# Eleven block products for twelve: Strassen's algorithm for pairs of output chunks in a q, k, v projection

## The chip, the cores and the metric

The kernel runs on one core of a Trainium2 chip. The metric is the device time of one execution in microseconds. Engines are named as in the profile: PE (TensorE), PEld (its weight loads), DVE (VectorE), ACT (ScalarE), POOL (GpSimd), SP (SyncE, here only a queue for transfers). Each has its own in-order queue; they meet at semaphores. On-chip memory is SBUF, the memory that TensorE writes to is PSUM[...].

## What is computed

Everything is float32. Two layers in a row on x of 384 channels and 192 x 192 pixels; this case concerns the first half of the first one:

```python
qkv = jnp.einsum('bchw,oc->bohw', gn(x), w_qkv) + b_qkv      # 384 -> 1152 channels, every pixel
qkv = qkv.reshape(b, 3*c, 96, 2, 96, 2).max(axis=(3, 5))      # 2 x 2 max pooling
qkv = depthwise_conv3x3(qkv, w_dw) + b_dw                     # on 96 x 96
q, k, v = split(qkv); q, k = normalized along the pixels
attn = q @ k.T * temperature                                  # 8 heads, 48 x 48
out = sum of four top-k softmaxes (k = 24, 32, 36, 38) of attn, each @ v * a_i
x = x + project(upsample(gelu(out)))
```

After it comes a second layer of depthwise convolutions (13 x 13 and six smaller ones, merged into one), on the normalized x.

## The kernel before, in words

**Tiling.** Channels are cut into chunks of 128: x has 3 (index j), the output has 9 (m: q is 0 to 2, k is 3 to 5, v is 6 to 8). Rows are cut into 24 blocks B of 8 input rows, each block into two halves (sb) of 4 input rows, 2 pooled rows. A half of a block and one output chunk is a *step*: it needs 2 x 384 columns (r = 0, 1: two input rows each) from 3 input chunks, six products of 128x128 by 128x384, summed in two PSUM banks (`project`, L665).

**Passes.** First x is read once for the statistics of the normalization (L301 to L585); what is already known of chunks 0 and 1 is used meanwhile for 18 early steps of blocks 0 to 5 (chunks m = 0 to 2, sb = 0), whose sums over j = 0, 1 are kept in SBUF (`put_by`) and put back into a bank by ACT just ahead of their step (`fill`, L264). Sums of 2 x 2 pixels of x (`sum_up`, L278) are made by POOL for a later stage; those of the early pieces that are left over are worked off at L636, behind the clearing of the nine padded tiles (L631 to L634). Then the q and k pass goes over the 24 blocks, 12 steps each (B 0 to 23), and the v pass once more over the same 24 blocks, 6 steps each (B 24 to 47), with the attention (`attend`, L797, mostly small DVE work) stepped on between its products. Then come the product of attention and v (L1131), the projection (L1459) and the second layer (L1371 to L1412).

**A step.** TensorE's six products; a DVE reduction takes the maximum over 2 x 2 pixels from the two banks (`pool`, L681 to L683); ACT adds the bias on the way into the padded tile of that chunk (L690). When both halves are there, ACT begins the depthwise sum with the middle tap (`begin`, L703), DVE adds the other eight taps (`taps`, L719), and ACT squares the result for the norms and copies the two last rows up (`end`, L733, L738). For q and k, TensorE transposes the result (`turn`, L748), ACT copies it (L750), and TensorE adds to the gram matrix (`add_gram`, L760).

**Order.** Nothing is reordered by a scheduler (`manual_schedule`): the order of the calls is the order on every engine's queue. The loop (L1006) issues a step's first product, then what is due at this step (`late`: begin one step after the second half, taps in two lots of four at two and three steps after, end and turn at four), the other five products, and `pool`. x of the next block is loaded at the start of a block (L1008), normalized by ACT from the seventh step on (L1031). PSUM: two tiles of two banks for the steps, gram 1, transposes 2, one bank for discarded squares.

Of the kernel before, what the change touches and what calls it, by code (L numbers as in the profile page):

```python
# [14 lines left out]
P = 128  # L15
C = 384
# [42 lines left out]
def tile_attn_then_large_kernel_conv(ctx: ExitStack, tc: tile.TileContext, a: dict, out: bass.AP):  # L59
# [161 lines left out]
    qkvps = ctx_a.enter_context(tc.tile_pool(name="qkvps", bufs=2, space=PSUM))  # L221
# [20 lines left out]
    o_spare = o  # L242
# [13 lines left out]
    assert (NJ * HS * WS - o) % FB >= 2 * SR * WS  # L256
    ring = [free[:, o + n * FB : o + (n + 1) * FB] for n in range((NJ * HS * WS - o) // FB)]
# [6 lines left out]
    def fill(B, m, sb):  # L264


        if sb == 0 and (B, m) in begun:
            ps = qkvps.tile([P, SR, 512], F32, tag="qkv", name="qkv")
            nc.scalar.copy(ps[:, :, : 2 * W], halved(begun[B, m]))
            filled.append(ps)  # L270
# [20 lines left out]
    with (  # L291
# [130 lines left out]
        def multiply(B, m, js, ps=None):  # L422

            start = ps is None
            if start:
                ps = qkvps.tile([P, SR, 512], F32, tag="qkv", name="qkv")
            for r in range(SR):
                for j in js:
                    nc.tensor.matmul(  # L429
                        ps[:, r, : 2 * W],  # L430
                        lhsT=wqk[:, j, m * P : (m + 1) * P],
                        rhs=pieces[B, 0, j][:, r * 2 * W : (r + 1) * 2 * W],
                        start=(start and j == js[0]),
                        stop=(j == js[-1]),
                        skip_group_check=not start,
                    )
            return ps
# [138 lines left out]
        whole = multiply(0, NJ, (0,))  # L576
        next(first)
        pc = in_one(last)
        multiply(0, NJ, (1,), whole)
        filled.append(whole)  # L580
# [12 lines left out]
    with ctx_v:  # L593
# [5 lines left out]
        trps = ctx_qk.enter_context(tc.tile_pool(name="trps", bufs=2, space=PSUM))  # L599
        jps = ctx_qk.enter_context(tc.tile_pool(name="jps", bufs=1, space=PSUM))  # L600
        wv = a2.tile([P, NJ, C], F32, name="wv")
        def load_v(c):
# [28 lines left out]
        for m in range(NM):  # L631
            pt = (a1 if m < 2 * NJ else a2).tile([P, R + 2, WS + 2], F32, name=f"pooled{m}")
            nc.gpsimd.memset(pt, 0.0)
            pool_t.append(pt)  # L634
# [9 lines left out]

        accs = {}
# [13 lines left out]
        def room():  # L659

            if filled:
                return filled.pop(), (NJ - 1,)
            return qkvps.tile([P, SR, 512], F32, tag="qkv", name="qkv"), range(NJ)

        def project(B, m, sb, ps, js):  # L665

            xt = xts[B, sb]
            wq, mm = (wqk, m) if m < 2 * NJ else (wv, m - 2 * NJ)
            for j in js:
                for r in range(SR):  # L670
                    nc.tensor.matmul(  # L671
                        ps[:, r, : 2 * W],
                        lhsT=wq[:, j, mm * P : (mm + 1) * P],
                        rhs=xt[:, j, r * 2 * W : (r + 1) * 2 * W],
                        start=(j == 0),
                        stop=(j == NJ - 1),
                        skip_group_check=(js[0] > 0),
                    )
                    yield

        def pool(m, sb, ps):  # L681
            mx = aw.tile([P, SR, WS], F32, tag="mx", name="mx", bufs=2)
            nc.vector.tensor_reduce(  # L683
                mx,
                ps[:, :, : 2 * W].rearrange("p r (y w x) -> p r w y x", y=2, x=2),
                AX.XY,
                ALU.max,
            )
            k = 2 + sb * SR
            nc.scalar.activation(  # L690
                pool_t[m][:, k : k + SR, 1 : 1 + WS], mx, AF.Identity, bias=bq[:, m : m + 1]
            )

        def begin(b, m):
# [5 lines left out]
            else:  # L700
                acc = a1.tile([P, R + 1, WS], F32, name=f"acc_{b}_{m}", tag="acc", bufs=8)
            accs[b, m] = acc
            nc.scalar.activation(  # L703
                acc[:, :na],
                pool_t[m][:, k0 + 1 : k0 + 1 + na, 1 : 1 + WS],
                AF.Identity,
                bias=bdw[:, m : m + 1],
                scale=wd[:, m, 4:5],
            )

        def taps(b, m, half):
# [3 lines left out]
            for t in ((0, 1, 2, 3), (5, 6, 7, 8))[half]:  # L715
                dy, dx = divmod(t, 3)

                nt = na if dy < 2 else n
                nc.vector.scalar_tensor_tensor(  # L719
                    acc[:, :nt],  # L720
                    pool_t[m][:, k0 + dy : k0 + dy + nt, dx : dx + WS],
                    wd[:, m, t : t + 1],
                    acc[:, :nt],
                    ALU.mult,
                    ALU.add,
                )

        def end(b, m):

            if m < 2 * NJ:  # L730
                na = rows(b)[2]
                junk = jps.tile([P, R + 1, WS], F32, name=f"junk_{b}_{m}", tag="junk")
                nc.scalar.activation(  # L733
                    junk[:, :na], accs[b, m][:, :na], AF.Square, accum_out=ssq[:, m, b : b + 1]
                )
            if b < NB - 1:
                pt = pool_t[m]
                nc.scalar.copy(pt[:, 0:2, 1 : 1 + WS], pt[:, R : R + 2, 1 : 1 + WS])  # L738

        def turn(b, i):  # L740
# [3 lines left out]
            for s in range(2):  # L744
                ps = trps.tile([P, C], F32, tag="tr", name="tr")
                for j in range(NJ):
                    acc = accs[b, s * NJ + j].rearrange("p r w -> p (r w)")
                    nc.tensor.transpose(ps[:n, j * P : (j + 1) * P], acc[:, i * P : i * P + n], ident)  # L748
                t = a1.tile([P, C], F32, tag=f"qk{s}", name=f"qk{s}")
                nc.scalar.copy(t[:n], ps[:n])  # L750
                qk.append(t)
            return qk, n, (b, i) == (0, 0), (b, i) == (NB - 1, chunks(NB - 1) - 1)
# [16 lines left out]
        def strip(n):  # L769
# [17 lines left out]
            for u in range(UQ):  # L787
                nc.gpsimd.dma_start(  # L788
                    out=bass.AP(
                        zd.tensor,  # L790
                        zd.offset + (u * 32 + c0) * ZS + u * BC,
                        [[UQ * 32 * ZS, P], [ZS, ZQ], [1, K0 * BC]],
                    ),
                    in_=z,
                )

        def attend(c1, c_ps):  # L797
# [4 lines left out]
            shid = c1.tile([P, 3 * P], F32, name="shid")  # L802
# [36 lines left out]
            rb = c1.tile([P, NJ, P2], F32, name="rb")  # L839
# [3 lines left out]
            rkp = c_ps.tile([P2, C], F32, name="rkp", tag="att")  # L843
            for j in range(NJ):
                nc.tensor.matmul(rkp[:, j * P : (j + 1) * P], lhsT=rb[:, j], rhs=ident, start=True, stop=True)
            rqp = c_ps.tile([P2, NPR], F32, name="rqp", tag="att")
# [11 lines left out]
            rk = c1.tile([P2, NPR, P2], F32, name="rk")  # L858
# [3 lines left out]
            nc.vector.tensor_copy(rqt, rqp)  # L862
            gs = c1.tile([P2, NPR, P2], F32, name="gs")
# [85 lines left out]
        late = {}  # L949

        def at(step, f, *args):
            late.setdefault(step, []).append((f, args))

        turned = []

        def turn_next(b, i):
            turned.append(turn(b, i))

        def gram_next():
# [656 lines left out]
```

## Time and profile before

| | us |
|---|---|
| time, median of 3 (lowest, highest) | 2869.0 (2866.7, 2895.1) |
| the profiled execution | 2862.9 |
| its span on the core | 2861.1 |
| statistics and early steps | 0 to 166 |
| q and k pass | 166 to 1334 |
| v pass | 1334 to 1906 |
| the rest (attention times v, projection, second layer) | 1906 to 2861 |

| stage | us | PE busy | DVE busy | ACT busy | POOL busy |
|---|---|---|---|---|---|
| q and k pass | 1168 | 1161.3 | 974.2 | 565.0 | 345.4 |
| v pass | 572 | 568.4 | 519.0 | 263.1 | 125.1 |

The profile page tells, for one execution, each engine's busy time; groups of instructions by source line with their count, mean duration and the idle time before them with what ended it; and the chain of work that ended last. Other views are the busy time in chosen stretches and the instructions in order of time. A matmul of float32 leaves two records, each with a weight load. Records of neighbours overlap a little, so the spacing is what a product costs, not its mean duration.

### The profile page before, as it was taken

Reading aid. Unit: us, or ns where it says so; the run is one execution under the profiler, and the core shown is the slowest. Engines: PE = TensorE matmul, PEld = TensorE weight load, DVE = VectorE, ACT = ScalarE, POOL = GpSimd, SP = SyncE. Lnnn points to the kernel's source line nnn. Section 1 sums busy time; section 2 is a strip of 40 time slices with the busy share of each in tenths; the row PEclk is TensorE's granted clock in tenths of the full one; section 3 lists DMA queues with packets and bytes.
Section 4 is the critical chain, followed back from the end, with each engine's and each line's share of the span. In section 5 each row is a group of like instructions: output and inputs, shape, how many; then the busy total and the mean of one; then the engine's idle time right before and its main releaser. Section 6 shows DMA issues by size and latency. Waiting matters only on the chain.

```text
span 2861.1 us, 37738 instructions
## 1 busy us (share of the span) xinstructions
PE 2735.6 (96%) x13662; PEld 1677.2 (59%) x13662; DVE 2498.5 (87%) x3484; ACT 1332.9 (47%) x2427; POOL 917.3 (32%) x1129
## 2 busy tenths in 40 slices
PE   0699999999999999999999999999999999999998
PEld 0356666666666666666655555545566666666666
DVE  6879998888878888788899998888789999999997
ACT  3755554444444444454444444444334444444443
POOL 4251231332323223241222222232114445444443
PEclk9899999999999999999999999999999999999999
DMA  9942432232422324232333333328889999999996
GB/s 389 419 151 65 134 114 87 81 126 72 135 74 92 111 70 137 67 126 81 100 108 107 108 109 116 115 69 234 234 206 282 270 275 275 256 271 271 270 275 168
DMA packets 269561, 475.75 MB, mean 166 GB/s; under 512 B 25858, under 2 KB 189968, under 8 KB 269248
## 3 DMA queue, kind: packets, MB, share of 16 engines
q1 hardware_dynamic: 204208, 301.51, 38.2%
q0 software_dynamic: 43328, 149.04, 15.5%
q10 hardware_dynamic: 21840, 22.81, 2.3%
q8 instruction: 108, 1.77, 0.3%
q14 instruction: 77, 0.63, 0.1%
HBM read 337.06 MB, written 136.20 MB: 165 GB/s over the span
## 4 chain that ended last, share of the span: by engine, by line
PE 85%; DVE 7%; DMA 5%; ACT 1%; issue 1%; POOL 0%; ACTq 0%; SPq 0%; DVEq 0%; POOLq 0%
PE qkv L671 51%; PE conv L1371 24%; PE pj L1459 4%; DVE v L719 3%; DMA xs<-in_x 3%; PE gram L760 2%; PE tr L748 2%; PE av L1131 1%; DVE mx L683 1%; PE qkv L429 1%; DVE acc L719 1%; DVE stats L535 1%; DMA v<-in_x 0%; DMA smj<-sums 0%; DMA wt<-zd 0%
## 5 line engine op out<-in xcount | busy, mean ns | idle before, releaser
L671 PE MATMUL qkv<-xt,wqk 128*128 128x384 f32 x3304 | 1082.5, 486 | 1.9 <-DVE mx L683 1.1
L671 PEld LDWEIGHTS qkv<-xt,wqk 128*128 128x128 f32 x3304 | 620.1, 190 | 417.1 <-DVE mx L683 4.5
L719 DVE SCALAR_TENSOR_TENSOR acc<-pooled,wd,acc 128x384 f32<-128x384 f32 (+2 forms) x1152 | 733.7, 637 | 30.6
L1371 PE MATMUL conv<-xp,wt 128*64 128x288 f32 (+1 forms) x6016 | 723.9, 404 | 2.4 <-issue 1.7
L690 ACT ACTIVATE pooled<-mx,bq 128x192 f32<-128x192 f32 x432 | 196.8, 456 | 900.2 <-DVE mx L683 898.1
L1371 PEld LDWEIGHTS conv<-xp,wt 128*64 128x64 f32 x6016 | 462.9, 137 | 260.8 <-issue 2.7
L683 DVE TENSOR_REDUCE mx<-qkv 128x192 f32<-128x768 f32 x432 | 412.3, 954 | 200.1 <-PE qkv L671 187.1
L671 PE MATMUL qkv<-xt,wv 128*128 128x384 f32 x1728 | 562.4, 487 | 2.5 <-DVE mx L683 2.2
L671 PEld LDWEIGHTS qkv<-xt,wv 128*128 128x128 f32 x1728 | 326.0, 190 | 233.4 <-DVE mx L683 9.8
L1351 DVE STREAM_TRANSPOSE xp<-xn 128x4608 f32<-128x4608 f32 (+1 forms) x107 | 445.4, 4163 | 18.0 <-PE conv L1371 10.6
L280 POOL TENSOR_TENSOR sum<-xt 128x192 f32<-128x192 f32 x128 | 87.9, 687 | 969.0 <-ACT xt L651 968.0
L719 DVE SCALAR_TENSOR_TENSOR v<-pooled,wd,v 128x384 f32<-128x384 f32 (+2 forms) x576 | 375.4, 652 | 15.2
L1379 ACT ACTIVATE co<-conv,cb 128x288 f32<-128x288 f32 x376 | 186.9, 497 | 386.1 <-PE conv L1371 381.3
L651 ACT ACTIVATE xt<-xt,gn 128x768 f32<-128x768 f32 x278 | 275.5, 1014 | 0.0
L1328 POOL TENSOR_TENSOR raw<-raw,up 128x2496 f32<-128x2496 f32 x46 | 230.0, 5001 | 38.2 <-DMA up<-pd 27.6
L1421 POOL DMA_DIRECT2D out<-o x194 | 107.4, 582 | 373.5 <-DVE o L1412 315.2
L1412 DVE STREAM_TRANSPOSE o<-co 128x2304 f32<-128x2304 f32 (+3 forms) x50 | 211.0, 4222 | 9.6 <-ACT co L1403 8.8
L1459 PE MATMUL pj<-v,wp 128*128 128x384 f32 x432 | 142.6, 489 | 1.0 <-ACT v L1138 0.7
L788 POOL DMA_DIRECT2D zd<-v x96 | 72.0, 756 | 216.1 <-ACT v L779 216.1
L1336 ACT ACTIVATE xn<-raw,par 128x2112 f32<-128x2112 f32 x48 | 103.1, 2148 | 25.4 <-POOL raw L1328 21.8
L1459 PEld LDWEIGHTS pj<-v,wp 128*128 128x128 f32 x432 | 80.9, 190 | 55.9 <-ACT v L1138 1.4
L281 POOL TENSOR_TENSOR sum<-sum,xt 128x192 f32<-128x192 f32 x128 | 100.9, 789 | 10.8
(296 smaller groups left out, 1914.6 us busy)
## 6 DMA issues: line engine op xcount, KB each, us to landing
xt<-in_x SPq DMA_DIRECT2D x96, 1152.0 KB, 7.4
raw<-in_x SPq DMA_DIRECT2D x182, 312.0 KB, 13.2
out<-o POOLq DMA_DIRECT2D x188, 288.0 KB, 8.4
wt<-zd SPq DMA_DIRECT2D x46, 1024.0 KB, 12.2
zd<-v POOLq DMA_DIRECT2D x96, 416.0 KB, 4.4
up<-pd SPq DMA_DIRECT2D x184, 156.0 KB, 12.6
xs<-in_x POOLq DMA_DIRECT2D x20, 768.0 KB, 10.7
smj<-sums SPq DMA_DIRECT2D x72, 192.0 KB, 3.0
```

The source lines that it names most:

```text
L651: nc.scalar.activation(xt[:, j], xt[:, j], AF.Identity, bias=gn0[:, j, 1:2], scale=gn0[:, j, 0:1])
L671: nc.tensor.matmul(ps[:, r, : 2 * W], lhsT=wq[:, j, mm * P : (mm + 1) * P], rhs=xt[:, j, r * 2 * W : (r + 1) * 2 * W], start=(j == 0), sto ...
L683: nc.vector.tensor_reduce(mx, ps[:, :, : 2 * W].rearrange("p r (y w x) -> p r w y x", y=2, x=2), AX.XY, ALU.max,)
L690: nc.scalar.activation(pool_t[m][:, k : k + SR, 1 : 1 + WS], mx, AF.Identity, bias=bq[:, m : m + 1])
L719: nc.vector.scalar_tensor_tensor(acc[:, :nt], pool_t[m][:, k0 + dy : k0 + dy + nt, dx : dx + WS], wd[:, m, t : t + 1], acc[:, :nt], ALU.mu ...
L1328: eng.tensor_add(rv, rv, uv.unsqueeze(2).to_broadcast([P, (m1 - m0) * WS, 2]))
L1351: nc.vector.transpose(bass.AP(at.tensor, at.offset, [list(at.ap[0]), [NBQ, n], [1, NBQ], [NQ * NBQ, CC], [ME * NBQ, NE]],), bass.AP(row.te ...
L1371: nc.tensor.matmul(ps[h * MH : (h + 1) * MH, t0:t1], lhsT=wt[:, c, o : o + MH], rhs=d[:, c, g + 2 * t0 : g + 2 * t1 - 1 : 2, :], start=(e ...
L1379: nc.scalar.activation(co[:, c], ps, AF.Identity, bias=cb[:, cc : cc + 1])
L1412: nc.vector.transpose(bass.AP(at.tensor, at.offset, [list(at.ap[0]), [2 * W, n], [BC, NBQ], [W, 2], [1, BC]]), bass.AP(of.tensor, of.offse ...
L1421: engines[u % len(engines)].dma_start(out=bass.AP(out.tensor, out.offset + k * CC * HW + (2 * u + t0 * BR) * W, [[ME * UQ * W, CC * NE], [ ...
L1459: nc.tensor.matmul(ps, lhsT=wp[:, j, i * P : (i + 1) * P], rhs=v[:, j, b * RB : (b + 1) * RB, :].rearrange("p r w -> p (r w)"), start=(j = ...
```

## The change

Take two output chunks m1, m2, two input chunks (j = 0, 1) and two columns of data: the upper and the lower input row y of a pooled row (for both pooled rows of a half block, so that a product has again 384 columns). That is a 2 x 2 by 2 x 2 product of blocks with a third input chunk beside it. The eight products of the 2 x 2 part are replaced by seven (Winograd's form of Strassen's algorithm), the four of the third chunk stay: eleven for twelve. The pairs are (3, 4), (0, 1), (2, 5) in the q and k pass, and (6, 7) in the v pass, where chunk 8 stays by itself (`single`). The early steps of chunks 0 to 2, sb = 0, stay as they were (`early_one`), and chunks whose partner is early are single there.

What is needed for it:

- *Sums of weights* s1 to s4 for each pair, four POOL instructions of 128x128 (`mix`), once a pair and pass.
- *Differences of data* t1 to t4 for each half block, four POOL instructions of 128x384 (`differ`). They are stored to DRAM and loaded again for the v pass (`differ_again`), on SP's queue.
- *Sums of products*: three times in a pair ACT copies a PSUM bank into another (`seed`), and TensorE goes on adding in both. Six single banks in a ring (`idle`) take the place of the two tiles. One more sum is made by POOL in SBUF.
- *The maximum*: the upper row's bank is moved to SBUF by ACT (`moved`), DVE takes the maximum with the lower row's bank (`larger`) and then of neighbouring columns, straight into the padded tile (`pool`). The bias is no longer added there: it goes into the bias of the middle tap (`shift_biases`), and the rim of the padded tiles is set to minus the bias by ACT (`pad`).
- *Order*: side work goes into four lists, ACT's (`acts`), DVE's taps (`taps_left`), TensorE's transposes and gram (`pes`), POOL's (`others`), from which a unit takes a fixed number at fixed places. The padded tiles are now cleared at the start of the loop's part, behind the remaining early sums. The padded tiles of v exist twice. Depthwise sums and other tiles move into unused parts of v's space; transposes have one bank.

The diff, cut to its core:

```diff
+        def mix(p, to=None):
+
+            s1, s2, s3, s4 = ((mixed[p] if to is None else to)[:, n] for n in range(4))
+            a11, a12, a21, a22 = (weights(m, k) for m in p for k in range(2))
+            yield nc.gpsimd.tensor_add(s1, a21, a22)
+            yield nc.gpsimd.tensor_sub(s2, s1, a11)
+            yield nc.gpsimd.tensor_sub(s3, a11, a21)
+            yield nc.gpsimd.tensor_sub(s4, a12, s2)
...
+        def differ(B, sb):
+
+            t1, t2, t3, t4 = (rows_of(diffs(B, sb)[:, n]) for n in range(4))
+            b11, b12, b21, b22 = (part(B, sb, j, y) for j in range(2) for y in range(2))
+            for t, p, q in ((t1, b12, b11), (t3, b22, b12), (t2, b22, t1), (t4, b21, t2)):
+                yield nc.gpsimd.tensor_sub(t, p, q)
+            differed.add((B, sb))
+            nc.sync.dma_start(out=tds[2 * B + sb], in_=diffs(B, sb).rearrange("p q n -> p (q n)"))
...
+        def product(n, w, xs, start=False):
+            assert start or n in used
+            used.add(n)
+            nc.tensor.matmul(
+                rows_of(banks[n]), lhsT=w, rhs=xs, start=start, stop=True, skip_group_check=True
             )
+
+        def seed(n):
+            k = idle.pop(0)
+            assert k in used
+            nc.scalar.copy(banks[k], banks[n])
+            return k
+
+        def moved(n, tag):
+
+            e = aw.tile([P, 2 * W], F32, tag=tag, name=tag, bufs=2)
+            nc.scalar.copy(e, banks[n])
+            idle.append(n)
+            return e
+
+        def larger(e, n):
+            nc.vector.tensor_tensor(e, banks[n], e, ALU.max)
+            idle.append(n)
...
+        def pair(B, p, sb):
...
+            def head():
+                n["a"] = idle.pop(0)
+                product(n["a"], weights(m1, 0), xs[0][0], True)
+                n["b"] = seed(n["a"])
+                act(2)
+                other(1)
+
+            def body():
+                product(n["b"], s2, t2)
+                n["c"] = seed(n["b"])
+                act(1)
+                product(n["a"], weights(m1, 1), xs[1][0])
+                product(n["a"], weights(m1, 2), xs[2][0])
+                e.append(moved(n["a"], "e1"))
+                act(1)
+                other(1)
+                aside(1)
+                n["e"] = idle.pop(0)
+                product(n["e"], s3, t3, True)
+                e.append(moved(n["e"], "e3"))
+                product(n["b"], s1, t1)
+                n["d"] = seed(n["b"])
+                act(1)
+                aside(1)
+                product(n["c"], weights(m2, 1), t4)
+                product(n["c"], weights(m2, 2), xs[2][0])
+                e.append(moved(n["c"], "e2"))
+                act(1)
+                tap(5)
+                while behind:
+                    behind.pop()()
+                tap(1)
+                other(1)
+
+            def tail():
+                product(n["d"], s4, xs[1][1])
+                tap(2)
+                product(n["d"], weights(m1, 2), xs[2][1])
+                larger(e[0], n["d"])
+                pool(B, m1, sb, e[0])
+                tap(1)
+                product(n["b"], weights(m2, 2), xs[2][1])
+                larger(e[2], n["b"])
+                nc.gpsimd.tensor_add(e[2], e[2], e[1])
+                behind.append(lambda: pool(B, m2, sb, e[2]))
+                aside(1)
...
         with ctx_m:
             variance = input_variance()
...
+            shift_biases(range(2 * NJ))
+            for m in (NJ, NJ + 1, NJ + 2, 0, 1, 2):
+                nc.gpsimd.memset(pool_t[m], 0.0)
+            for m in (NJ, NJ + 1, NJ + 2, 0, 1, 2):
+                acts.append((0, 1, lambda m=m: pad(m)))
+            act(1)
+            for _ in mix(PAIRS[0]):
+                pass
+            for _ in differ(0, 1):
+                pass
...
+            for now, (B, u, kind, what, sb) in enumerate(units):
...
+                head, body, tail = kind(B, what, sb)
+                head()
                 if attention:
                     next(attention[0], None)
+                if before:
+                    before()
+                hook(B, u, len(units_of(B)))
+                body()
...
+                before = tail
```

`before` is the tail of the unit before: a unit's first product stands ahead of the last three of its forerunner. `hook` loads x of the next block at a block's first unit, normalizes it in the last four units of a block (q and k pass), and puts `differ` and the sums into POOL's list.

## The prediction

> **What bounds the kernel now.** I read the page's busy line first, then the stage table (busy time in stretches), then the groups by line, and last the order of time where the stages join.
>
> ```profile
> PE 2735.6 (96%) x13662; PEld 1677.2 (59%) x13662; DVE 2498.5 (87%) x3484; ACT 1332.9 (47%) x2427; POOL 917.3 (32%) x1129
> ```
>
> TensorE has hardly any idle time, and VectorE is not far behind. So the stages are looked at one by one; columns are the stretch, then busy time of PE, PEld, DVE, ACT and POOL, the clock, the DMA share and GB/s.
>
> ```profile
> 317.00:361.00 44.00, 42.97 (x165) 26.59 (x163) 40.48 (x61) 25.41 (x53) 10.17 (x13) 1.00 0.34 109
> 503.50:554.00 50.50, 50.50 (x188) 31.29 (x187) 40.98 (x61) 23.45 (x50) 13.91 (x20) 1.00 0.28 95
> 1490.00:1547.00 57.00, 54.64 (x162) 29.11 (x160) 54.45 (x117) 22.92 (x38) 11.45 (x18) 1.00 0.29 92
> 1700.00:1800.00 100.00, 100.00 (x312) 58.92 (x311) 90.27 (x130) 45.37 (x76) 24.59 (x38) 1.00 0.34 107
> ```
>
> The first is one early block of the q and k pass (B 1 to 5), the second one of its 18 full blocks, the third a part of the v pass that carries the attention between its products, the fourth the plain v pass. A full block is TensorE's alone (DVE 41.0 of 50.5 us). An early block has DVE at 40.5 of 44, the v pass at 90%, and beside the attention at 96% with TensorE's own rate down (162 matmul records in 57 us where 312 in 100 is normal).
>
> ```profile
> L671 PE MATMUL qkv<-xt,wqk 128*128 128x384 f32 x3304 | 1082.5, 486 | 1.9 <-DVE mx L683 1.1
> L719 DVE SCALAR_TENSOR_TENSOR acc<-pooled,wd,acc 128x384 f32<-128x384 f32 (+2 forms) x1152 | 733.7, 637 | 30.6
> L690 ACT ACTIVATE pooled<-mx,bq 128x192 f32<-128x192 f32 x432 | 196.8, 456 | 900.2 <-DVE mx L683 898.1
> L683 DVE TENSOR_REDUCE mx<-qkv 128x192 f32<-128x768 f32 x432 | 412.3, 954 | 200.1 <-PE qkv L671 187.1
> ```
>
> One product of 128x128 by 384 columns is two records (3304 + 1728 = 2 x 2516 products). The chain that ended last has 12 records in 3.87 us, so a product is 0.645 us. A full block is 72 x 0.645 = 46.5 us, plus about 4 us of transposes and gram: the 50.5 of the table.
>
> [...] in the v pass: four taps take 2.57 us alone and 3.44 us where POOL adds beside them.
>
> ```profile
> 1599.80 2.57 DVE L719 SCALAR_TENSOR_TENSOR v<-pooled,wd,v 128x384 f32<-128x384 f32 x4
> 1607.54 3.44 DVE L719 SCALAR_TENSOR_TENSOR v<-pooled,wd,v 128x384 f32<-128x384 f32 x4
> 1608.90 0.79 POOL L281 TENSOR_TENSOR sum<-sum,xt 128x192 f32<-128x192 f32 x1
> ```
>
> So POOL's adding costs DVE about a quarter of POOL's time (0.63 to 0.85 us a tap, the same 0.22 us lost in 0.85). [...]
>
> **The change part by part.**
>
> *Products.* Pairs of chunks take 11 products a half block in place of 12. Pair units: 18 full blocks x 6 = 108, block 0 has 3, blocks 1 to 5 have 4 each, together 131 in the q and k pass; the v pass has 24 x 2 = 48. So 179 x 0.645 = 115.5 us of TensorE goes: 6 x 0.645 = 3.9 us a full block (50.5 to 46.6), 1.3 us a v block (23.2 to 21.9).
>
> *ACT.* A pair unit gets three seeds (bank to bank) and three moves (bank to SBUF) of 128x384: 6 x 0.48 = 2.9 us. The bias write L690 goes (2 x 0.456). Full block: 23.45 + 36 x 0.48 - 12 x 0.456 = 35.3 of 46.6 us. The throughput is there; the question is order. The seed lies in TensorE's own chain: product, seed, product into the copy. After the first product come the previous unit's three tail products, 1.9 us, before the copy is used; seed c has the two a products and e between (1.9 us), seed d the two c products and the next first one. A seed with its handovers is about 0.8 us (0.48 and some 0.15 on either side, like ACT qk after PE tr), so 1.1 us is left for what stands ahead of it in ACT's queue, usually one activation of 0.34 to 1.01 us. I put 0.15 us of wait a unit. A seed's bank-to-bank copy has no row of this shape: 0.43 (overlapped copy) to 0.58 (L1467) bounds it.
>
> *DVE.* The reduce (954 ns) becomes a maximum of bank and moved half (0.544, from gram L864) and a maximum of neighbours (0.346, L1328 at 128x192): 0.89. That is nothing gained: the taps stay. POOL now reads SBUF more: per full block 8 differences and 6 sums of 384 columns at 0.9 us (between 0.75, by 2.0 ns an element, and 1.04, twice the 0.52 of 192) = 12.6 us, a quarter of it lost by DVE, with taps running some 80% of the time: +2.6 us. DVE full block: 41.0 - 0.8 + 2.6 = 42.8 of 46.6 us. A pair unit is then 7.1 us of TensorE (7.8 with gram) and about 7.3 of DVE, which has in its order to wait for TensorE twice. Together with the seeds I put a full block at 47.8, not 46.6: 2.7 x 18 = **49 us gained**.
>
> *Early blocks.* DVE 40.5 - 0.8 + 2.7 = 42.4 against TensorE's 38.7 + 4 - 2.6 = 40.1: DVE is the bound, the block goes from 44 to about 43: 5 x 1 = **5 us**.
>
> *v pass* (1334 to 1906, 572 us). TensorE: 557.7 - 31 + 7 for gram and attention = 534. DVE: 519 busy, minus 144 x 0.06, plus 48 sums x 0.9 x 0.25 = 11, about 521 of 534, and in the some ten blocks with attention it is over TensorE's rate: some 2 us of its small operations a block on 21.3. I put 14 us for these and 6 us of misses in the others: 554, **18 us gained** (bounds 5 and 30).
>
> *The start.* This is where the order is changed against itself. Now POOL first clears the padded tiles, and only then works off the early sums:
>
> ```profile
> 166.29 15.79 PE L671 MATMUL qkv<-xt,wqk 128*128 128x384 f32 x48
> 165.07 4.82 POOL L633 MEMSET pooled<- 128x588 f32 x9 [2.90 <-ACT v L440]
> 169.87 0.50 POOL L280 TENSOR_TENSOR v<-xt 128x192 f32<-128x192 f32 x1
> ...
> 189.78 0.56 POOL L284 DMA_DIRECT2D sums<-v  x1 [0.30 <-POOL v L282]
> ```
>
> After the change the sums come first on POOL (they could start at 162.2): 7 sums in 169.87 to 190.3 are 20 us, so to 182. Then 6 clearings x 0.54 = 3.2, mix of the first pair 4 x 0.4 = 1.6, and t1, t3, t2 at 0.9 = 2.7: t2 is there at about 189.5. ACT's pad waits for the first clearing at 182, and behind it stand the first moves and the put-back for the next early unit, on which DVE waits. TensorE has only 11 products (7.1 us, to 173.4) before it needs s2 x t2. **Lost: 16 us** (8 if the sums drain sooner, 20 if not), and DVE, the next bound, loses it too.
>
> *DMA.* 48 stores and 48 loads of 786 KB on SP's queue: 75 MB, at 30% DMA share in these stages. Stores stand before the next block's x loads and wait for POOL; x lands in 7.9 us and is needed two pair units (15 us) later: nothing on the path, at most 2 us a block if POOL is late. *The end.* More taps are left behind the last product (up to 24, some 15 us, against 11 us now). The av stage covers them if its tiles don't wait: 0 to 12 us, I take 4.
>
> Sum: 49 + 5 + 18 - 16 - 4 = 52. The profiled execution took 2862.9 us (span 2861.1): **2811**. The median of the runs shown, 2869.0, is 6 us above this execution; I give 2812.
>
> **Rivals.** *All of it is kept*: no waits, start hidden, 2863 - 115 + 4 to 15: about 2755 to 2765. For it: ACT and POOL have room. Against it: DVE's 96% beside attention, POOL's order at the start. *DVE becomes the bound*: contention twice as dear, differences at 1.1 us; a pair unit is 8 x 0.643 + 1.8 + 1.15 = 8.1 us of DVE, a full block 48.6, 18 x 1.9 = 34; early blocks nothing, v pass 6, less 20: **2843**. *Slower: the seeds' handshake.* One place, ACT's queue between product and seed: if a normalisation (1.01 us) or an act that waits for a late tap usually stands ahead, the three seeds of a pair cost TensorE some 0.3 us each, 0.9 x 179 = 161 us: 2863 - 115 + 20 + 161 = **about 2929**. It decides from (115 - 20) / 179 = 0.53 us a pair on. For it: ACT in order at 76%; against it: 1.9 us of other products over each seed, and six banks in turn. *That twelve stay*: the counts above exclude it.
>
> **How the numbers follow.** Forecast 0.50 (own range 2780 to 2838), all kept 0.12, DVE bound 0.24, handshake 0.14. Low 2770 lets most of "all kept" out, high 2862 takes in DVE's case and little of the handshake, so some 2 in 10 stay out. One per cent, about what a measurement of this kernel can tell from no change, is 28.7 us (below 2840, above 2898): faster takes 0.47 of the forecast, 0.12 and 0.09 of DVE's case, 0.68; within 0.20; slower 0.12.
>
> **What would show it.** A matmul count 358 lower. Full blocks of 47 to 48.5 us with TensorE over 96% and DVE over 90%; the sort of wait named for TensorE there being ACT's seed or DVE's maximum. Early blocks near 43 with DVE in front. TensorE idle between 174 and 189 for POOL. The v pass near 554, DVE at 97%. I am wrong if taps average over 0.75 us, if TensorE waits more than 0.5 us a pair unit for seeds, or if ACT's normalisation waits for x.

## The result, and the profile after

The changed kernel takes 3437.6 us (3436.8 to 3439.8, 4 runs) beside 2868.3 of the kernel before on the same chip: a ratio of 1.196 (95% interval 1.189 to 1.203). The profiled execution's span is 3435.0 us, 573.9 above the 2861.1 of before. The forecast was 2812, and none of its rivals came near: the slowest was 2929.

The stages say where it lies. The q and k pass takes 166 to 1752, 1586 us for 1168; the v pass 1752 to 2466, 714 for 572; the rest 969 for 955. So 418 + 142 + 14 = 574. From the page: the engines, and the groups that answer to those shown of before (mean in ns, then the idle time of the engine just before them and what ended it).

```profile
PE 2863.8 (83%) x13304; PEld 1604.0 (47%) x13304; DVE 2654.8 (77%) x3929; ACT 1667.4 (49%) x3195; POOL 1360.7 (40%) x1523
L991 DVE SCALAR_TENSOR_TENSOR v<-pooled,wd,v 128x384 f32<-128x384 f32 (+2 forms) x1440 | 1064.3, 741 | 360.0 <-ACT v L968 328.0
L748 PE MATMUL qkv<-xt,wqk 128*128 128x384 f32 x1818 | 732.7, 524 | 150.4 <-ACT qkv L755 59.9
L841 POOL TENSOR_TENSOR e<-e,e 128x384 f32<-128x384 f32 x179 | 217.9, 1217 | 1091.7 <-DVE e L766 960.2
L761 ACT COPY e<-qkv 128x384 f32<-128x384 f32 x611 | 291.2, 477 | 626.8 <-PE qkv L748 614.4
L755 ACT COPY qkv<-qkv 128x384 f32<-128x384 f32 x537 | 251.2, 468 | 437.7 <-PE qkv L748 333.6
L766 DVE TENSOR_TENSOR e<-qkv,e 128x384 f32<-128x384 f32 x432 | 238.4, 552 | 237.4 <-PE qkv L748 227.5
L783 DVE TENSOR_TENSOR pooled<-e 128x192 f32<-128x192 f32 x360 | 168.1, 467 | 21.7 <-POOL e L841 14.4
```

Matmul records are 13304 for 13662, 358 fewer, two for each of the 179 products: the work did go. Yet no engine is full: TensorE went from 96 to 83% busy, VectorE from 87 to 77%. TensorE's products, which had 1.9 us of idle time in front of 1082 us before, now have 150 in front of 733, and ACT's copies out of the banks wait 614 and 334 us for TensorE. All wait for one another. In the stage table (PE, PEld, DVE, ACT, POOL busy, clock, DMA share, GB/s) the start, a stretch of the early blocks, and full blocks of q and k (the stretch and its length stand first):

```profile
166.00:200.00 34.00, 16.10 (x41) 7.77 (x41) 3.49 (x8) 9.52 (x26) 30.46 (x52) 0.80 0.13 52
317.00:361.00 44.00, 34.54 (x114) 18.50 (x112) 34.95 (x55) 25.25 (x53) 13.45 (x14) 0.92 0.25 79
700.00:1000.00 300.00, 246.57 (x777) 131.80 (x777) 214.91 (x342) 154.70 (x325) 138.20 (x150) 0.92 0.27 92
```

TensorE is busy 246.6 of 300 us, at a granted clock of 0.92. Between 500 and 1100 us DVE does 431 taps, where before did 572:

```profile
L719 DVE SCALAR_TENSOR_TENSOR acc<-pooled,wd,acc 128x384 f32<-128x384 f32 x572 | 364.1, 637 | 15.2
L991 DVE SCALAR_TENSOR_TENSOR v<-pooled,wd,v 128x384 f32<-128x384 f32 x431 | 336.1, 780 | 129.4 <-ACT v L968 120.2
```

At 48 taps a full block that is 600 x 48 / 431 = 66.8 us a block, for 50.3. (The same count gives the block length of every run below.) Of the waits of the whole run, those around the banks, with their sum, number and longest:

```profile
ACT e L761 <- PE qkv L748: 614.4, 418, 6.6
DVE v L991 <- ACT v L968: 349.8, 133, 7.8
ACT qkv L755 <- PE qkv L748: 333.6, 282, 4.5
PEld qkv L748 <- DVE e L766: 250.0, 150, 4.7
PEld qkv L748 <- ACT qkv L755: 247.6, 173, 3.4
PEld qkv L748 <- ACT e L761: 200.2, 202, 16.4
DVE e L766 <- PE qkv L748: 227.5, 147, 18.6
```

TensorE waits for ACT's seeds (L755), for ACT's moves (L761) and for DVE's maxima (L766), 1.0 to 1.7 us each time; ACT and DVE wait for TensorE. That is a circle, and a piece of it in order of time shows how it turns:

```profile
902.20 0.30 PEld L748 LDWEIGHTS qkv<-v 128*128 128x128 f32 x2 [3.02 <-DVE e L766]
903.21 0.46 ACT L755 COPY qkv<-qkv 128x384 f32<-128x384 f32 x1 [3.98 <-PE qkv L748]
905.43 0.48 ACT L761 COPY e<-qkv 128x384 f32<-128x384 f32 x1 [0.82 <-PE qkv L748]
905.97 0.50 PEld L748 LDWEIGHTS qkv<-v 128*128 128x128 f32 x2 [1.72 <-ACT e L761]
908.99 0.46 ACT L755 COPY qkv<-qkv 128x384 f32<-128x384 f32 x1 [0.80 <-PE qkv L748]
909.36 0.71 ACT L968 ACTIVATE v<-pooled,shifted,wd 128x384 f32<-128x384 f32 x1
909.50 0.50 PEld L748 LDWEIGHTS qkv<-v,wqk 128*128 128x128 f32 x2 [1.75 <-ACT qkv L755]
910.10 0.62 DVE L991 SCALAR_TENSOR_TENSOR v<-pooled,wd,v 128x384 f32<-128x384 f32 x1 [2.56 <-ACT v L968]
```

TensorE gets on at 902.20 when DVE has let go of a bank; ACT has waited 3.98 us for its product and seeds; TensorE waits for ACT's move, then at 909.50, ahead of product c, for seed d, which product c does not read. ACT's begin of a depthwise sum (L968) stands behind all this in ACT's queue, so DVE's first tap waits 2.56 us for it, and DVE's next maximum, which frees a bank, comes later for that.

The question is why TensorE waits at all, with six banks and, by the order of the code, other products over each seed. The names in the built program answer it. Here is one unit of q and k as TensorE issues it, with the instruction whose semaphore it waits for (`qkv1.0` is the first bank of tile qkv1):

```
product b += s2 t2  into qkv1.1   waits for ACT's seed qkv1.1 <- qkv1.0
product a           into qkv1.0   waits for ACT's seed qkv0.0 <- qkv1.1
product e  = s3 t3  into qkv2.1   waits for DVE's maximum with qkv2.0
product b += s1 t1  into qkv1.1   waits for ACT's move of qkv1.0
```

Only the first is a wait for its own operand. The six "single banks" of the change are halves of three tiles:

```python
        banks = [t[:, r, : 2 * W] for t in ones for r in range(SR)]
```

and the three others wait for something that touches *the other bank of the same tile*. Product a, which was to lie over seed c, stands behind seed c. Which products are caught changes with the place in the ring: followed through a full block by the order of the code, product a stands behind seed c in three of the six units, and product c behind seed d in four, as at 909.50 above. Of TensorE's 1115 waits for ACT or DVE at these banks, 960 concern only the other bank of the tile.

### The profile page after: what moved, and what is told of

Read it like the earlier page. It is cut to its first block, busy times and chain, and to the rows that moved or that the text cites. A ratio compares the mean times of both kernels' runs of the same rounds, so it can differ in the third digit from the quotient of the medians.

```text
span 3435.0 us, 39405 instructions
## 1 busy us (share of the span) xinstructions
PE 2863.8 (83%) x13304; PEld 1604.0 (47%) x13304; DVE 2654.8 (77%) x3929; ACT 1667.4 (49%) x3195; POOL 1360.7 (40%) x1523
## 3 DMA queue, kind: packets, MB, share of 16 engines
q0 software_dynamic: 43328, 149.04, 13.3%
## 5 line engine op out<-in xcount | busy, mean ns | idle before, releaser
L991 DVE SCALAR_TENSOR_TENSOR v<-pooled,wd,v 128x384 f32<-128x384 f32 (+2 forms) x1440 | 1064.3, 741 | 360.0 <-ACT v L968 328.0
L748 PE MATMUL qkv<-xt,wqk 128*128 128x384 f32 x1818 | 732.7, 524 | 150.4 <-ACT qkv L755 59.9
L841 POOL TENSOR_TENSOR e<-e,e 128x384 f32<-128x384 f32 x179 | 217.9, 1217 | 1091.7 <-DVE e L766 960.2
L761 ACT COPY e<-qkv 128x384 f32<-128x384 f32 x611 | 291.2, 477 | 626.8 <-PE qkv L748 614.4
L748 PEld LDWEIGHTS qkv<-xt,wqk 128*128 128x128 f32 x1818 | 348.8, 200 | 460.1 <-ACT qkv L755 108.9
L748 PE MATMUL qkv<-xt,wv 128*128 128x384 f32 x1152 | 425.4, 500 | 91.8 <-DVE e L766 41.2
L755 ACT COPY qkv<-qkv 128x384 f32<-128x384 f32 x537 | 251.2, 468 | 437.7 <-PE qkv L748 333.6
L766 DVE TENSOR_TENSOR e<-qkv,e 128x384 f32<-128x384 f32 x432 | 238.4, 552 | 237.4 <-PE qkv L748 227.5
L748 PEld LDWEIGHTS qkv<-xt,wv 128*128 128x128 f32 x1152 | 209.9, 191 | 284.3 <-DVE e L766 73.6
L748 PE MATMUL qkv<-diff,v 128*128 128x384 f32 x444 | 191.0, 536 | 64.2 <-DVE e L766 44.8
L1688 POOL TENSOR_TENSOR raw<-raw,up 128x2496 f32<-128x2496 f32 x46 | 231.7, 5037 | 27.6 <-DMA up<-pd 23.2
L991 DVE SCALAR_TENSOR_TENSOR v<-wqk,wd,v 128x384 f32<-128x384 f32 (+1 forms) x288 | 194.5, 680 | 28.4 <-ACT v L968 21.8
L748 PE MATMUL qkv<-v 128*128 128x384 f32 x372 | 161.4, 538 | 59.7 <-DVE e L766 42.2
L748 PE MATMUL qkv<-diff,wqk 128*128 128x384 f32 x396 | 163.6, 513 | 25.8 <-ACT qkv L755 14.2
L783 DVE TENSOR_TENSOR pooled<-e 128x192 f32<-128x192 f32 x360 | 168.1, 467 | 21.7 <-POOL e L841 14.4
```

The source lines that it names most:

```text
L748: nc.tensor.matmul(rows_of(banks[n]), lhsT=w, rhs=xs, start=start, stop=True, skip_group_check=True)
L755: nc.scalar.copy(banks[k], banks[n])
L761: nc.scalar.copy(e, banks[n])
L766: nc.vector.tensor_tensor(e, banks[n], e, ALU.max)
L841: nc.gpsimd.tensor_add(e[2], e[2], e[1])
L991: nc.vector.scalar_tensor_tensor(acc[:, :nt], pooled(b, m)[:, k0 + dy : k0 + dy + nt, dx : dx + WS], wd[:, m, t : t + 1], acc[:, :nt], ALU ...
```

## The experiments

Theory A: the built program keeps its waits by the tile, so the products that should cover a seed stand behind it. Rival B, of the forecast: the seed's own handshake is slow, whatever the tiles. Rival C: POOL's work beside DVE costs far more than forecast.

**Six tiles of one bank.** With the banks each a tile, block 0's first early unit of chunk 3 becomes a single one (six products instead of two kept sums and a rest), since its half-done sum lay in a tile of two.

```diff
-        ones.append(more_ps.tile([P, SR, 512], F32, name="qkv2"))
+        ctx_e.close()
+        ones = [more_ps.tile([P, 512], F32, name=f"bank{n}") for n in range(6)]
...
-        banks = [t[:, r, : 2 * W] for t in ones for r in range(SR)]
+        banks = [t[:, : 2 * W] for t in ones]
```

> The changed kernel with its six PSUM banks declared as six tiles of one bank, where it has three tiles of two banks; nothing else in the order of the work changes, but for the one early unit whose sums stood in a two-bank tile: block 0's chunk 3, sb 0, is now a whole single unit. Theory A (waits are kept per tile, so a product into one bank waits for ACT's and DVE's use of the other bank of its tile, and the products that were to cover a seed stand behind it): the waits for ACT's moves and DVE's maximum at the seeds' places go, a full block falls from 69 us to 47 to 50, the whole to 2800 to 2900 us. Rival B (the true handshake product, seed, product is what costs): all those waits stay, above 3250 us. Rival C (POOL's reading slows DVE and everything waits for DVE): above 3250 us too.

2956.3 us, a ratio of 1.030 (1.027 to 1.033) to before; the span falls from 3435.0 to 2952.5, by 482.5 of the 573.9 us. TensorE has 872 waits at the banks in the program, and one that concerns a neighbour alone. Theory A holds for the larger part, and B falls as its cause: seeds and moves are the same, only the false waits went, and the chip did without them. But the time lies above A's 2800 to 2900 us: 91 us stay, and the table shows another bound; below it groups of 500 to 1100 us:

```profile
700.00:1000.00 300.00, 281.41 (x1015) 164.27 (x1014) 292.88 (x436) 197.42 (x428) 193.08 (x204) 1.00 0.36 122
```

```profile
L990 DVE SCALAR_TENSOR_TENSOR v<-pooled,wd,v 128x384 f32<-128x384 f32 x555 | 451.5, 813 | 20.0 <-ACT v L967 8.2
L840 POOL TENSOR_TENSOR e<-e,e 128x384 f32<-128x384 f32 x70 | 86.3, 1233 | 198.9 <-DVE e L765 165.9 <-PE bank L747 13.9 <-ACT xt L685 11.9
L782 DVE TENSOR_TENSOR pooled<-e 128x192 f32<-128x192 f32 x139 | 80.2, 577 | 2.4
L730 POOL TENSOR_TENSOR diff<-xt,diff 128x384 f32<-128x384 f32 x24 | 31.6, 1316 | 0.0
```

DVE is busy 97.6%. A tap takes 813 ns where it took 637 in the same stretch of before, a maximum of neighbours 577 where I had priced 346. Beside them POOL's sums take 1.23 us and its differences 1.31, where I had priced 0.9 (my 2.0 ns an element was from before: L1328 on POOL, 5001 ns for 2496 columns). A block takes 600 x 48 / 555 = 51.9 us.

**POOL light, with the two-bank tiles kept.** POOL's differences are left out from block 4 on, and its sums of moved parts everywhere, so that the output lacks these parts.

```diff
-                yield nc.gpsimd.tensor_sub(t, p, q)
+                yield nc.gpsimd.tensor_sub(t, p, q) if B < 4 else None
...
-                nc.gpsimd.tensor_add(e[2], e[2], e[1])
```

> The changed kernel with its three two-bank tiles, but POOL's differences are left out from block 4 on (the tiles keep what stands in them, the stores and loads stay) and the sum of two moved banks on POOL is left out everywhere, so 14 instructions of 1.2 us a full block less; the output isn't the reference's. Rival C (contention and POOL's lateness) expects the larger part of the loss back: below 3150 us. Theory A and rival B expect taps of 0.64 us in place of 0.78 but the same waits between TensorE, ACT and DVE: 3300 to 3420 us.

3420.7 us (1.192, 1.187 to 1.197; 2 runs), only 17 less. Taps fall to 638 ns, and the block is as long as ever (433 taps in 600 us, 66.5 us):

```profile
L990 DVE SCALAR_TENSOR_TENSOR v<-pooled,wd,v 128x384 f32<-128x384 f32 x433 | 276.2, 638 | 189.2 <-ACT v L967 180.0
```

Rival C falls for the change as it stands: VectorE's lost time is hidden behind the circle.

**POOL light and six tiles.** The two edits together; the same parts of the output are missing.

> Six tiles of one bank, and on POOL the differences of x left out from block 4 on and the sum of two moved parts left out everywhere (so the output lacks these parts). Theory A2 (what is left of the loss once each bank is a tile of its own is POOL's reading beside DVE): taps fall from 0.81 to below 0.68 us, a full block from 51.4 to 46.8 to 48.5 us, the whole to 2850 to 2885 us. Rival B2 (the seeds' handshake still sets the block): the block stays above 50 us, the whole above 2920 us, whatever the taps do.

2814.3 us, 0.981 of before (0.979 to 0.984), span 2813.2: further down than the 2850 to 2885 expected.

```profile
700.00:1000.00 300.00, 298.51 (x1108) 182.79 (x1107) 257.25 (x468) 216.67 (x466) 101.07 (x136) 1.00 0.42 137
```

TensorE is busy 298.5 of 300 us and the block takes 600 x 48 / 613 = 47.0. So the seeds do lie under other products once each bank is a tile, and POOL's work is worth 2952.5 - 2813.2 = 139 us there, but 17 behind the false waits. Taken away in this order, the spans make the whole difference: 482.5 (false waits) + 139.3 (POOL) - 47.9 (what is then still gained on before, with that work of POOL unpaid) = 573.9.

**The third tile split alone**, nothing else touched: a part of the first edit, to see whether it brings its part of the gain.

```diff
-        ones.append(more_ps.tile([P, SR, 512], F32, name="qkv2"))
+        split = [more_ps.tile([P, 512], F32, name=f"bank{n}") for n in range(2)]
...
+        banks = [t[:, r, : 2 * W] for t in ones for r in range(SR)] + [t[:, : 2 * W] for t in split]
```

> The change as it is, but the third tile of two banks split into two tiles of one bank, the other two left. In the built program 655 of TensorE's 1026 waits on ACT or DVE at the banks then concern the other bank of a tile alone; they are 960 of 1115 in the change, 1 of 872 with six tiles. Theory A (waits kept by the tile): a part of the gain of six tiles, in proportion 481 x 305 / 960 = 150 us: 3200 to 3350 us. Rival D (something else that went with the six tiles, as the unit of block 0 made anew or where the banks lie): 3420 to 3440 us.

3277.1 us (1.143, 1.140 to 1.147), 160 us less for 305 false waits less; expected were 150. The two runs differ by 22 us, and the profiled one is the longer: its q, k and v passes are 170 us shorter than the change's, and the rest 21 longer. Rival D, something else that came with the six tiles, falls: block 0 is as in the change here.

**The banks numbered across the tiles**, a test that told nothing.

```diff
-        banks = [t[:, r, : 2 * W] for t in ones for r in range(SR)]
+        banks = [t[:, r, : 2 * W] for r in range(SR) for t in ones]
...
-        idle = [n for n in (4, 0, 1, 2, 3, 5) if n // SR != begun_in]
+        idle = [n for n in (2, 0, 3, 1, 4, 5) if n % 3 != begun_in]
```

> Tiles of two banks as in the change, but the six banks numbered across the three tiles, so that banks taken one after the other are of different tiles. Theory A (waits are kept by the tile): some of the waits on a neighbour bank fall away and others come, so the time changes by over 50 us, and lies between 2960 and 3600 us. Rival (six small allocations differ from three large ones in something else than the neighbour): within 20 us of 3437 us.

3434.4 us, one run: unchanged. My expectation missed, and the fault is in the edit. A seed may only take a bank that a product has written (the kernel's `assert k in used`), and the ring's first order, so chosen and written out, is the same order of banks under other numbers; it is a repeat of the change, and evidence neither for nor against the rival.

**The differences and sums on DVE**, six tiles.

```diff
-                yield nc.gpsimd.tensor_sub(t, p, q)
+                yield nc.vector.tensor_sub(t, p, q)
...
-                nc.gpsimd.tensor_add(e[2], e[2], e[1])
+                nc.vector.tensor_add(e[2], e[2], e[1])
```

> Six tiles, and the differences of x and the sums of moved parts made by DVE in place of POOL: 14 operations of some 0.56 us a full block, 7.8 us more work on DVE. Theory A2 (contention): DVE wins back more than that, since its taps return to 0.65 us and its maxima of neighbours to 0.35 (11 us a block): DVE some 48 to 49.5 us a full block, the whole 2880 to 2925 us. Rival C2 (DVE is simply full and POOL's reading costs it nothing): 7.8 us come on top of 51.4, the whole is 3060 to 3100 us.

2880.2 us (1.004, 1.002 to 1.007): 76 us less than with POOL, though DVE has 14 instructions more a block. Taps are back at 649 ns, neighbours at 382, DVE at 96.3% and the block at 49.5:

```profile
L990 DVE SCALAR_TENSOR_TENSOR v<-pooled,wd,v 128x384 f32<-128x384 f32 x582 | 377.7, 649 | 20.5 <-ACT v L967 8.0
L782 DVE TENSOR_TENSOR pooled<-e 128x192 f32<-128x192 f32 x145 | 55.4, 382 | 2.5
```

The rival, that DVE is simply full and POOL costs it nothing (3060 to 3100), falls. POOL's work cost DVE more than doing it does: against this run POOL's 6 sums at 1.23 and 8 differences at 1.31 us (17.9 us a block) took 48 x (0.813 - 0.649) + 12 x (0.577 - 0.382) = 10.2 us from VectorE, 0.57 us for each us of POOL, while VectorE itself needs 14 x 0.60 = 8.4. Its maxima with a bank, one input in PSUM, take 549 ns in both. **The sums alone on DVE**, differences left on POOL:

> Six tiles, and only the sums of moved parts (6 a full block, 2 a block of the v pass) made by DVE, the differences of x left on POOL. If each operation of POOL costs DVE 0.8 us and DVE's own 0.56, this gives 6 x 0.24 = 1.5 us a full block and as much for each sum in the v pass, so some 35 to 45 us in all: 2910 to 2922 us. If it is the order (VectorE's maximum of neighbours waits for POOL's sum) that costs more than the reading, it gives nearly all of the 76 us of the run with both on DVE: 2880 to 2895 us. If the differences alone do the harm, 2945 to 2960 us.

2913.3 us (1.017, 1.016 to 1.019), 43 of the 76 us for six of the fourteen operations a block and all 48 in the v pass. That is the price by the operation (35 to 45 expected); had the wait of the maximum of neighbours for POOL's sum been the larger part, nearly all of the 76 would have come. Taps take 747 ns and neighbours 439, together 5.4 us a block more than with both on DVE, for 8 differences of 1.18 us on POOL: again 0.57 for each.

**A dose on the kernel before.** Nothing of the change, and 14 additions on POOL in each block of q and k that nobody reads.

```diff
+                for _ in range((2 if u % 6 == 0 else 1) if B < NB else 0):
+                    nc.gpsimd.tensor_add(extra, extra, extra)
```

> The kernel before, with nothing of the change, and 14 additions of a 128x384 scratch tile to itself on POOL in each of the 24 blocks of the q and k pass; nobody reads them. Theory A2 (POOL's reading costs VectorE about 0.65 us for each us): each is some 1.2 us, VectorE loses 11 us a block, so that its 41 become 52 of a block of 50.5 us: the full blocks 52 to 53.5 us, the early ones 50 to 52 for 44, taps about 0.80 us, the whole 2925 to 2965 us. The price of the forecast (0.9 us each, a quarter lost): VectorE 44 of 50.5, taps 0.69, the whole 2863 to 2875 us.

3010.2 us (1.051, 1.049 to 1.054). Its groups between 500 and 1100 us:

```profile
L719 DVE SCALAR_TENSOR_TENSOR acc<-pooled,wd,acc 128x384 f32<-128x384 f32 x514 | 412.5, 803 | 13.6
L1028 POOL TENSOR_TENSOR extra<-extra 128x384 f32<-128x384 f32 x154 | 145.7, 946 | 8.9
L683 DVE TENSOR_REDUCE mx<-qkv 128x192 f32<-128x768 f32 x128 | 121.7, 951 | 65.4 <-PE qkv L671 65.4
```

Taps of 803 ns are what was expected, and without a line of the change. The reduction, with its input in PSUM, takes 951 for the 956 of before in this stretch. POOL's operation is cheaper here than I put (946 ns; it reads the same data twice, where the change's reads two inputs; that this is why was not tried), so a block loses 48 x (0.803 - 0.637) = 8.0 us on DVE for 13.2 us of POOL, 0.6 for each. The time missed: 146 us for the 60 to 100 expected. A block takes 56.0 us with DVE busy only 85%, so full throughput was the wrong thing to compare with. TensorE's weight loads wait 27.6 of the 600 us for DVE's reductions and 26.3 for its last taps, where before has next to none, and its granted clock is 0.96 for 1.00. The additions come in runs (eight in a row in 8.35 us at 803), which may be why; it was not tried.

**The start.** First the left-over sums behind the clearing and the first mixture:

```diff
-        while early_sums:
-            sum_one()
...
             for _ in differ(0, 1):
                 pass
+            while early_sums:
+                sum_one()
```

> As the six-tile kernel, and POOL's leftover early sums stand behind the clearing of the padded tiles, the first pair's sums of weights and the first differences, as POOL's other work at the start. The stall of TensorE between about 174 and 190 us should go: 12 to 18 us less than the six-tile kernel by every theory, if that stall is POOL's order at the start; no difference if ACT or the loads hold the start.

2954.5 us (1.030, 1.026 to 1.033): no gain. The stall had only moved:

```profile
191.73 0.50 PEld L745 LDWEIGHTS bank<-diff,v 128*128 128x128 f32 x2 [9.66 <-POOL v L706]
200.77 0.36 DVE L780 TENSOR_TENSOR pooled<-e 128x192 f32<-128x192 f32 x1 [19.13 <-POOL e L838]
```

TensorE now waits 9.66 us for the next pair's mixture (L706), which still stood behind the sums, and DVE 19 us for POOL's sum of moved parts behind all of them. Then the sums behind all mixtures, with the differences on DVE:

> As the run before it, and POOL's left-over early sums put behind all the mixtures of weights at the start. If the stall at the start is POOL's order alone, 12 to 18 us less than the run before it; if it only moves again (as when one mixture still stood behind the sums), within 4 us of it.

2868.7 us (1.0013, 1.0000 to 1.0025), 11.5 less, just under the 12 to 18 expected. TensorE is busy 31.5 of the 34 us from 166 to 200, as before the change (32.1), for 19.7 without the edit; before first, then this run:

```profile
166.00:200.00 34.00, 32.06 (x99) 18.14 (x98) 27.88 (x41) 15.34 (x31) 23.24 (x39) 1.00 0.20 48
166.00:200.00 34.00, 31.51 (x91) 17.59 (x90) 26.08 (x51) 16.29 (x43) 25.32 (x43) 0.95 0.17 67
```

**The end.** Both pair units of the last block ahead of its single ones.

```diff
-                return [(pair, vs, 0), (single, 2 * NJ + 2, 0), (pair, vs, 1), (single, 2 * NJ + 2, 1)]
+                k = ((pair, vs, 0), (single, 2 * NJ + 2, 0), (pair, vs, 1), (single, 2 * NJ + 2, 1))
+                return [k[n] for n in ((0, 2, 1, 3) if B == 2 * NB - 1 else range(4))]
```

> Six tiles, differences and sums on DVE, the start in the new order, and in the last block of the v pass both pair units ahead of the two single ones, so that 16 of the 24 last taps fall beside products. If the 12 us by which the part after the v pass is longer than before are DVE's taps behind the last product, 4 to 9 us less than the 2868.7 of the run without it: 2859 to 2865 us. If the weight preparation and halo copies there set it, no difference (2867 to 2871 us).

2869.5 us (1.0011, 0.9998 to 1.0025): no difference, the value of the second branch, though not for its reason. DVE runs 95% busy through the v pass (1400 to 1850 us) and behind TensorE at its end; another order of the units takes no work out of its queue. Its last tap ends 22.2 us after the last product of v with the edit (1897.3 to 1919.5) and 23.2 without; before the change it was 11.1. DVE is busy 19.40 of the 20 us from 1900 to 1920 in both, where before had 13.84 from 1904 to 1924. So the taps left behind do match the 12 us in size, but the edit hardly took them away; that they set all of the 12 was not shown.

**Two pairs of three.**

```diff
-                return [(pair, p, sb) for p in (kv, q01, rest) for sb in range(2)]
+                return [(pair, p, sb) for p in (kv, q01) for sb in range(2)] + [
+                    (single, m, sb) for m in rest for sb in range(2)
+                ]
```

> As the run before it, and only two of the three pairs of q and k made by eleven products, the third as two single chunks in the full blocks (all differences stay; 36 products come back, of which 2 a full block, 1.3 us; DVE loses 2 sums of 0.56 us). If DVE, at 96 to 97 per cent, sets the full block (48.6 to 49.4 us), the block falls to some 48 us, 8 to 16 us off the run before it: 2845 to 2856 us. If TensorE is the nearer bound or the single units' own waits cost more, it is 5 to 25 us slower than the run before it.

2913.4 us (1.016, 1.015 to 1.018), 44 us slower than the run before it: the second branch, and more than it said. The block is 51.6 us, and TensorE (94%) and DVE (92%) both have gaps. The wait that grew is TensorE's for ACT's copies of the transposes, ahead of the gram products: 40.7 us of 600 in its weight loads, for 13.3. A single unit also takes one of the transposes' places more (needed so that depthwise sums come free in time); which of the two edits costs the time was not tried apart.

No version here beats the kernel before, except the one that leaves POOL's work out, and with it a part of the output.

## Why the prediction was wrong, step by step

*The step that failed* is under ACT: "seed c has the two a products and e between (1.9 us), seed d the two c products and the next first one ... I put 0.15 us of wait a unit." I read the cover from the order of the calls and did not ask on what a product waits. The code names its banks as slices of two-bank tiles, and with that product a waits for seed c itself in half of the units, product c for seed d in more, and others for moves and maxima at a neighbour. A pair unit of q and k takes about 66.8 / 6 = 11.1 us for the 8.0 that I put, and 8.7 with six tiles; over the two passes the false waits are worth 482 us where the forecast put 0.15 x 179 = 27. Two of the three signs of being wrong that I had named are there: taps of 780 ns in full blocks, and 247.6 / 179 = 1.4 us a pair of waiting for seeds. The rival "handshake" had the right place, ACT between product and seed, and the wrong mechanism: it looked for long instructions in ACT's queue, and its 0.53 us a pair was passed for another reason. With the false waits gone, the original judgement holds: the block is 47.0 us in the run with POOL light, where 46.6 are products and transposes.

*The mis-sized term* is DVE's loss: "12.6 us, a quarter of it lost by DVE ... +2.6 us". With six tiles it is 17.9 us of POOL and 10.2 us lost a block: longer operations, and 0.57 for each us; the dose has 0.60. The quarter was a misreading. I divided what four taps lost by how long they took, as if POOL had added all the while; but beside those four taps, from 1607.54 to 1610.98, it adds only three times, the 0.79 us that I showed and

```profile
1608.30 0.52 POOL L280 TENSOR_TENSOR sum<-xt 128x192 f32<-128x192 f32 x1
1609.77 0.80 POOL L282 TENSOR_TENSOR sum<-sum,xt 128x192 f32<-128x192 f32 x1
```

So 3.44 - 2.57 = 0.87 us were lost to 2.11 us of adding, 0.41 for each: this stretch of before already shows about half of the gap, if it is one stretch alone. With POOL's work as it is, the six-tile version goes from 48 us ahead of before to 91 behind. Which of DVE's instructions pay, the dose on before shows: taps, with their inputs in SBUF, go from 637 to 803 ns, and the reduction, with its input in PSUM, takes 951 for 956. How much they pay, 0.57 to 0.60, is what these runs show.

*Right:* the count (358 records). The start, near enough: TensorE is busy 16.1 of 34 us for 32.1, where I put 16 us lost; but it is 22.3 with six tiles, whose block 0 also has more products of its own, so that not all of the 16 need be POOL's order. There 11.5 came back with POOL's order changed, once the differences were DVE's; that moving the sums behind the first mixture would do was wrong. The sum of the rest: with six tiles and POOL light the span is 2813 where the steps made 2811. That it is so near is luck: the q and k pass is 44 us shorter (my 49 + 5 - 16 = 38), the v pass 17 (my 18), the end 13 longer (my 4), and the run doesn't pay for the work of POOL that my steps count. *The end*: in the change 12 us from the last product of v on (968 for 957), in the six-tile versions 11 to 14, but for one whose profiled run was 7 us above its others; I put 4 of a range to 12. DVE's queue is full for 22 us behind the last product, 11 before. *DVE as the bound* (2843) is what happens with six tiles, at 2953: the mechanism was right, and its "contention twice as dear" was four times (10.2 us a block for 2.6).

## What to carry to other kernels

Before you count on an instruction to cover a wait, look up what *it* waits for, and in which unit your program keeps waits: here two PSUM banks in one tile were one thing to wait for, and a ring of six was a ring of three. When work moves from the bound engine to an idle one, price what it does to the third: here 17.9 us of POOL's additions took 10.2 from VectorE, more than the 8.4 that it needs to do them itself. And an edit whose two costs hide one another (17 us for POOL's work with the circle there, 139 with it gone) needs both removed together before either can be judged.

## What the runs showed of the hardware

- POOL's additions beside DVE cost VectorE 0.57 us (two inputs read, six-tile runs) to 0.60 us (the same data read twice, the dose) for each us. The instructions that grew have their inputs in SBUF: taps from 637 to 803 ns under the dose, and in the six-tile runs, POOL's work on DVE against on POOL, taps from 649 to 813 and maxima of neighbours from 382 to 577. Those with an input in PSUM stayed within 5 ns: the reduction 956 and 951, the maximum with a bank 549 in both. Whether POOL's reads or its writes do it was not tried apart.
- A 128x384 float32 addition or subtraction on POOL took 0.95 us where it read the same data twice (the dose, DVE 85% busy) and 1.11 to 1.32 us where it read two inputs (six tiles, with and without the sums on DVE; DVE 98 and 96% busy).
- TensorE's granted clock from 700 to 1000 us was 0.92 where it was busy 82% of the time (the change), 0.97 at 85% (third tile split) and 1.00 at 94% (six tiles), but also 0.96 at 93% (the dose) and 0.97 at 96% (sums alone on DVE): the busy share by itself does not order it. What grants it was not tried. From 500 to 1100 us the records of a product (L748, x and weights as they are) took 528 ns in the change, at a clock of 0.93, for 486 before, at 1.00; that the clock is why was not shown, for with the sums alone on DVE groups of 486 and of 541 ns stand in one stretch.
